# Gathered rows' buffers placed under the node stage, and relu of every second node tile on ScalarE, in a graph-network layer

## The chip, the cores and the metric

One core of one Trainium2 chip. The metric is the device time of one execution in microseconds; the kernel before took 4068.4 us, the median of three runs (4061.18 to 4073.2). The core's engines appear under the profile's names: PE (TensorE, matmuls; PEld its weight loads), DVE (VectorE), ACT (ScalarE), POOL (GpSimd) and SP (SyncE, which here only issues DMAs). A "q" behind a name (ACTq, SPq) is that engine's instruction queue, where DMA issues stand.

## The reference, cut to what matters

A message-passing layer over N = 12,500 nodes with 160 features (64 scalars and 32 vectors of 3) and E = 400,000 edges sorted by target.

```python
h = jnp.maximum(_layernorm(x, axis=-1), 0.0)
...
x0 = node_input[:, :MUL0]
x1 = node_input[:, MUL0:].reshape(n, MUL1, 3)
s0 = x0 @ W_sc0 * a * inv0
y0 = x0 @ W_l1_0 * a * inv0
y1 = jnp.einsum('nuc,uv->nvc', x1, W_l1_1) * a[:, :, None] * inv1
h = jax.nn.silu(edge_length_embedded @ fc_W1 * (1.0 / math.sqrt(FC_IN)))
w = h @ fc_W2 * (1.0 / math.sqrt(FC_H))
ys0 = y0[edge_src]
ys1 = y1[edge_src]
...
z0 = jnp.zeros((n, MID), mid0.dtype).at[edge_dst].add(mid0) * inv_nb
z1 = jnp.zeros((n, MID, 3), mid1.dtype).at[edge_dst].add(mid1) * inv_nb
...
return x + concat(C_S * s + C_X * (z @ W_l2) * a)
```

(The last line is shortened.) Each node's features are normalized and clipped at zero, then mapped by two weight matrices: s stays with the node, y is what neighbours read. Each edge gathers the y row of its source node, multiplies it by weights from a small network over the edge's attributes, and the products are summed at the target node. The division by the standard deviation is applied after the maps, as a factor on each row, so what has to be formed ahead of the maps is relu(x - mean) alone.

## The kernel before, in words

**Node stage (lines 267 to 410).** The 98 node tiles of 128 rows are worked in groups of 8 (GN), a group in steps of 2 tiles (HN). After them come 40 more tiles (RT), whose rows are not read in order but gathered from x into `xr` by the edges' source indices: they are the rows that 10 of the later edge blocks will need, mapped here a second time. They are called the reuse groups below. A step goes through seven stages, each some iterations behind the first: `center` (DVE: bn_stats, bn_aggr, then h = max(x - mean, 0), for either tile of the step; at the end of a group ACT takes the square root `ra` of the variances), `turn_rows` (PE transposes h), `out_of_psum` (ACT copies hT), `map_rows` (PE, two matmuls per tile), `leave` (ACT writes ys = po x ra; at the end of a group ACT issues the store of y to DRAM, `y_d` for the node groups and `yr_d` for the reuse groups), `scales` (DVE turns ra into its reciprocal times the node's attribute) and `add_s` (DVE adds s onto acc, L384, for the node groups). In one iteration q the stages are issued in the order scales(q-1), leave(q-4), out_of_psum(q-2), turn_rows(q-1), map_rows(q-3), center(q), add_s(q-5), and PE, ACT and DVE keep that order (`manual_schedule`). POOL and SP are ordered by the framework. On POOL lie the 80 gathers of `xr` and `ar` and the all-reduce L136 that finds the first target node of every window of edges.

**relate (lines 138 to 181).** DVE work of some 24 us on the edges' targets, after the last step. Its largest tile is `over`.

**Edge stage (lines 436 to 654).** 3125 edge tiles of 128 edges, in 782 blocks of 4. For a block b: `load(b)` gathers 4 x 128 rows of y_d into a buffer of the pool `yg` (POOL, one indirect DMA per tile, L474); every twelfth block from 12 to 120 is instead one plain load from yr_d, issued by SP (L471). `load` also issues, on SP, the edge attributes `xe` (L465), for every eighth block. `weigh` makes the edge weights (PE, then ACT scales them, L421), `select` and `products` (DVE, L427 to L434) multiply them with the gathered rows, `sums` (PE) adds up by target. A buffer of yg is free again when the products of its block have read it (L432 is the last to do so). Ten loads are issued ahead of the loop (AHEAD), then load(b + 10) in iteration b, and the pool has 12 buffers.

**Memory.** Pools are laid one upon the other in the order in which they are opened, and what a closed pool leaves is used again; whoever first writes to such memory waits for the last use of what lay there. Above the constants (from byte 114,912 of a partition on) lie, one after the other in time: idx, then the node stage's pools (xr at 138,528 to 164,128, the two ys buffers at 164,928 to 185,408), then relate's (over at 148,000 to 160,544, above idx), then the edge stage's (selp, prod, xe at 151,776 to 155,872, raw to 158,944, ev to 162,784, and yg at 162,784 to 193,504, 12 buffers of 2,560 bytes, then hid and post).

Of the kernel before, what the change touches and what calls it, by code (L numbers as in the profile page):

```python
# [10 lines left out]
F32 = mybir.dt.float32  # L11
I32 = mybir.dt.int32
AF = mybir.ActivationFunctionType
ALU = mybir.AluOpType
# [4 lines left out]
P = 128  # L19
# [26 lines left out]
def kernel(  # L46
# [19 lines left out]
    nc = tc.nc  # L66
# [51 lines left out]
    tile_i = const.tile([P, NG], I32, name="tile_i")  # L118
    far_i = const.tile([1, 1], I32, name="far_i")
    full = T // WT  # L120
    before = ctx.enter_context(ExitStack())
    ip = before.enter_context(tc.tile_pool(name="idx", bufs=1))
    dst_i = ip.tile([P, TP], I32, name="dst_i")
# [143 lines left out]
    with (  # L267
# [43 lines left out]
        def rows_of(g, n):  # L311
            return acc[:, g:g + n, :] if g < NT else xr[:, g - NT:g - NT + n, :]

        def center(q):

            g, n, j, m = steps[q]
            xt = rows_of(g, n)
            if j == 0:
                mvs[g] = ns.tile([P, GN, 2], F32, name="mv")
            mv = mvs[g]  # L320
            h = nd.tile([P, HN, D], F32, name="h")
            for k in range(m):
                st = ns.tile([P, 6], F32, name="st")
                nc.vector.bn_stats(st, xt[:, j + k, :])
                nc.vector.bn_aggr(mv[:, j + k, :], st)
                nc.vector.tensor_scalar(h[:, k, :], xt[:, j + k, :], mv[:, j + k, 0:1], 0.0, ALU.subtract, ALU.max)
            hs[q] = h
            if j + m == n:
                ra = ns.tile([P, GN], F32, name="ra")
                nc.scalar.activation(ra[:, :n], mv[:, :n, 1], AF.Sqrt, bias=eps)  # L330
                ras[g] = ra
# [55 lines left out]
        with tc.manual_schedule(engines=engines):  # L387
            load_x(0, HN)
            nc.sync.dma_start(a_sb, attr)
            node_weights()  # L390
            load_x(HN, min(GN, NT) - HN) if NT > HN else None
            nc.sync.dma_start(src_sb, src)
            for k, (g, n) in enumerate(groups[1:]):
                load_x(g, n)
                if k == 4:
                    nc.sync.dma_start(dst_i, dst)
            if len(groups) <= 5:
                nc.sync.dma_start(dst_i, dst)
            edge_weight_loads()
            last = len(steps) - 1  # L400
            mid = len(steps) - -(-RT // HN)
            for q in range(len(steps) + 5):
                if q == min(4, last) and RT:
                    gather_x()
                if q == min(16, mid):
                    first_nodes()
                for stage, lag in ((scales, 1), (leave, 4), (out_of_psum, 2), (turn_rows, 1), (map_rows, 3), (center, 0),
                                   (add_s, 5)):
                    if 0 <= q - lag <= last:
                        stage(q - lag)  # L410
# [25 lines left out]
    with (  # L436
# [1 line left out]
        tc.tile_pool(name="prod", bufs=3) as prod,  # L438
        tc.tile_pool(name="ld", bufs=2) as ld,
        tc.tile_pool(name="ev", bufs=2) as evp,  # L440
        tc.tile_pool(name="yg", bufs=12) as ygp,
        tc.tile_pool(name="hid", bufs=4) as hid,
        tc.tile_pool(name="post", bufs=2) as post,
        tc.tile_pool(name="p_w", bufs=2, space=PSUM) as p_w,
# [171 lines left out]
        with order:  # L616
# [10 lines left out]
            for b in range(NB):  # L627
                g, k = divmod(b, K)
# [30 lines left out]
    with (  # L659
# [11 lines left out]
        with tc.For_i(0, n, 1) as _:  # L671
            with tc.For_i(0, ZR, P) as r:
                nc.sync.dma_start(z_d[ds(r, P), :], zero)
            with tc.For_i(0, TP // GT, 1) as g:
# [15 lines left out]
                yg = fp.tile([P, GT, D], F32, name="f_yg")  # L690
# [102 lines left out]
```

## Time and profile before

| | |
|---|---|
| three runs | 4061.18, 4068.4, 4073.2 us |
| the profiled execution | 4061.72 us, of it span 4059.8 us |
| busy: PE, DVE, ACT, POOL | 3235.3, 2922.8, 2692.2, 3018.0 us (80, 72, 66, 74% of the span) |
| mean granted TensorE clock | 0.933 |
| node stage, first to last `center` | 11.9 to 166.3 us |
| relate on DVE | 166.8 to 190.8 us |
| first products on DVE | 208.0 us |
| gathers on POOL, first and last start | 175.2 and 4039.1 us |

How to read it: a group row gives the line, engine and operation, names (out<-in) and a count, then the busy time and the mean duration in ns, then the idle time of the engine just ahead of those instructions and what ended most of it. A row of the timeline gives the start, the busy time, engine, line and operation; in brackets stands the engine's idle time ahead of it and whom the profile names as the releaser. "issue" is time in which the engine waited for nothing that the profile shows. The releaser is inferred, and a wait for several things is put down to the one that came last. Rows of stretches of time give begin and end, the length, then the busy time of PE, PEld, DVE, ACT and POOL (with counts), the granted clock, the DMA engines' mean busy share, and GB/s.

### The profile page before, as it was taken

The numbers are of one execution on the slowest core, as the hardware profiler recorded it, in microseconds if no ns is written. First come the engines' busy times: TensorE is split into PE (matmuls) and PEld (weight loads), VectorE is DVE, ScalarE is ACT, GpSimd is POOL, SyncE is SP. The second block draws the span as 40 slices with busy tenths as digits, with TensorE's granted clock in tenths as the row PEclk, the third lists the DMA queues.
The fourth block names the chain that finished last, engine by engine and source line by source line (L and its number), as shares of the span: only waits on it lengthen the run. The fifth ranks groups of instructions, "written<-read, shape, count | busy, mean of one in ns | idle before, by whom it ended". The sixth has DMA issues, their size and how long they took to land.

```text
span 4059.8 us, 62554 instructions
## 1 busy us (share of the span) xinstructions
PE 3235.3 (80%) x17505; PEld 2347.5 (58%) x17505; DVE 2922.8 (72%) x7558; ACT 2692.2 (66%) x9543; POOL 3018.0 (74%) x3177
## 2 busy tenths in 40 slices
PE   6588888878787787887877887878777788778777
PEld 5466666555555555555555555555555555555555
DVE  7787777776777777777777777767777777777776
ACT  5477777766666666666666666666666666666665
POOL 7477777777777777777777777777777777777776
PEclk9899999999989989999999999999999989999998
DMA  6333333332322233323233332323232323243233
GB/s 192 88 84 83 80 83 80 76 76 74 77 74 74 74 76 74 77 74 76 72 76 75 75 76 74 74 74 77 74 76 74 76 72 76 75 124 75 72 81 78
DMA packets 244949, 326.49 MB, mean 80 GB/s; under 512 B 67290, under 2 KB 194342, under 8 KB 244342
## 3 DMA queue, kind: packets, MB, share of 16 engines
q0 software_dynamic: 151280, 256.22, 25.7%
q1 hardware_dynamic: 74322, 54.52, 4.7%
q10 hardware_dynamic: 18996, 11.72, 0.9%
q8 instruction: 141, 2.31, 0.2%
q14 instruction: 210, 1.72, 0.1%
HBM read 302.92 MB, written 19.28 MB: 79 GB/s over the span
## 4 chain that ended last, share of the span: by engine, by line
DVE 25%; POOL 23%; DMA 21%; issue 21%; PE 5%; ACT 1%; DVEq 1%; ACTq 0%; POOLq 0%
POOL yg L474 23%; DMA yg<-y_d,src_sb 21%; DVE tmp L429 5%; DVE tmp L427 5%; DVE pr L432 3%; DVE pr L431 2%; DVE acc L603 2%; DVE pr L434 2%; DVE sel L538 2%; PE pz L556 2%; DVE pr L430 2%; DVE sel L536 1%; PE pw L505 1%; PE px L483 1%; DVE place L586 1%
## 5 line engine op out<-in xcount | busy, mean ns | idle before, releaser
L474 POOL DMA_INDIRECT yg<-y_d,src_sb x3085 | 2925.3, 948 | 982.5 <-issue 745.8
L556 PE MATMUL pz<-pr,sel 128*128 128x256 f32 x6250 | 1623.9, 407 | 0.3 <-DVE pr L434 0.3
L421 ACT ACTIVATE pw<-pw,ev 128x96 f32<-128x96 f32 x3125 | 985.3, 315 | 858.3 <-PE pw L505 769.6
L556 PEld LDWEIGHTS pz<-pr,sel 128*128 128x128 f32 x6250 | 1237.4, 208 | 157.6 <-issue 0.9
L505 PE MATMUL pw<-w,hT 64*128 64x192 f32 x6250 | 758.5, 363 | 667.1 <-DVE pr L434 657.5
L427 DVE TENSOR_TENSOR tmp<-yg,pw 128x384 f32<-128x384 f32 x782 | 432.8, 553 | 972.3 <-DMA yg<-y_d,src_sb 970.8
L505 PEld LDWEIGHTS pw<-w,hT 64*128 64x128 f32 x6250 | 514.6, 194 | 1060.9 <-DVE pr L434 893.9
L563 ACT ACTIVATE zs<-pz 32x64 f32<-32x64 f32 x3126 | 669.9, 214 | 41.8
L429 DVE TENSOR_REDUCE tmp<-tmp 128x128 f32<-128x384 f32 x782 | 463.7, 593 | 27.0
L538 DVE TENSOR_TENSOR sel<-sel,pw 128x384 f32<-128x384 f32 x782 | 432.7, 553 | 27.0
L561 ACT ACTIVATE zs<-pz 32x192 f32<-32x192 f32 x1042 | 337.8, 324 | 148.3 <-PE pz L556 125.7
L432 DVE TENSOR_TENSOR pr<-pw,yg 128x384 f32<-128x384 f32 x782 | 428.8, 548 | 0.0
L483 PE MATMUL px<-xe,w 32*128 32x512 f32 x782 | 301.0, 656 | 81.8 <-issue 72.7
L488 ACT ACTIVATE hT<-px 128x512 f32<-128x512 f32 x391 | 218.5, 595 | 179.8 <-PE px L483 172.9
L431 DVE TENSOR_TENSOR pr<-pw,yg 128x256 f32<-128x256 f32 x782 | 324.1, 414 | 0.0
L430 DVE TENSOR_TENSOR pr<-pw,yg 128x256 f32<-128x256 f32 x782 | 323.8, 414 | 0.0
L536 DVE TENSOR_TENSOR sel<-iota,pw 128x128 f32<-128x128 f32 x782 | 218.8, 280 | 58.0 <-ACT pw L422 57.6
L580 PE MATMUL px<-wc,za 128*128 128x96 f32 (+1 forms) x1566 | 257.3, 305 | 0.4 <-ACT za L573 0.4
L580 PEld LDWEIGHTS px<-wc,za 128*128 128x128 f32 x1566 | 211.6, 205 | 62.2 <-issue 45.2
L434 DVE TENSOR_TENSOR pr<-pw,tmp 128x128 f32<-128x128 f32 x782 | 220.4, 282 | 0.0
L594 PE MATMUL px<-os,place 128*128 128x160 f32 x1044 | 219.0, 334 | 0.5 <-ACT os L583 0.5
L603 DVE SCALAR_TENSOR_TENSOR acc<-px,a_sb,acc 128x160 f32 x522 | 198.5, 380 | 12.2 <-PE px L594 2.7
(97 smaller groups left out, 1742.0 us busy)
## 6 DMA issues: line engine op xcount, KB each, us to landing
yg<-y_d,src_sb POOLq DMA_INDIRECT x3085
xe<-in_e SPq DMA_DIRECT2D x784, 32.0 KB
y_d<-ys ACTq DMA_DIRECT2D x12, 640.0 KB
acc<-in_x SPq DMA_DIRECT2D x11, 640.0 KB
out<-acc SPq DMA_DIRECT2D x11, 640.0 KB
raw<-in_e SPq DMA_DIRECT2D x32, 192.0 KB
yr_d<-ys ACTq DMA_DIRECT2D x5, 640.0 KB
yg<-yr_d SPq DMA_DIRECT2D x10, 320.0 KB
```

The costliest lines, as they stand in the source:

```text
L421: nc.scalar.activation(pw[:, k, 0:96], pw[:, k, 0:96], AF.Copy, scale=ev[:, k, 0:1])
L427: nc.vector.tensor_tensor(tmp[:, :n, 0:3, :], y1, wt[:, :n, NW:NW + 3].unsqueeze(3).to_broadcast([P, n, 3, M1]), ALU.mult)
L429: nc.vector.tensor_reduce(tmp[:, :n, 3, :], tmp[:, :n, 0:3, :].rearrange("p t c u -> p t u c"), AX.X, ALU.add)
L430: nc.vector.tensor_mul(pr[:, :n, 192:PC], wt[:, :n, 96:160], yg[:, :n, 0:M0])
L431: nc.vector.tensor_mul(pr[:, :n, 0:M0], wt[:, :n, 0:M0], yg[:, :n, 0:M0])
L432: nc.vector.tensor_mul(pr[:, :n, 96:192].rearrange("p t (c u) -> p t c u", c=3), wt[:, :n, M0:96].unsqueeze(2).to_broadcast([P, n, 3, M1]) ...
L474: nc.gpsimd.indirect_dma_start(out=yg[:, k, :], out_offset=None, in_=y_d, in_offset=bass.IndirectOffsetOnAxis(ap=src_sb[:, t:t + 1], axis=0))
L505: nc.tensor.matmul(pw[:, k, 0:NW], hT[r, o:o + P], w2[r, :], start=True, stop=True)
L538: nc.vector.tensor_tensor(sel[:, :, 0:3, :], sel[:, :, 3:4, :].to_broadcast([P, n, 3, WN]), wt[:, :n, NW:NW + 3].unsqueeze(3).to_broadcast ...
L556: nc.tensor.matmul(pz[:, 0:PC], sels[g][:, t % TG, :, :], pr[:, k, :], start=t % WT == 0, stop=last)
L563: nc.scalar.activation(zs[:, 192 + M0 * c:192 + M0 * (c + 1)], pz[WN * c:WN * (c + 1), 192:PC], AF.Copy)
L580: nc.tensor.matmul(po[:m, lo:hi], za[:, k, :m], wc[:, k, lo:hi], start=k == 0, stop=k == 1)
```

## The change

The pool `yg` is opened ahead of `idx` and so lies right above the constants for the whole program, under the memory of idx, the node stage and relate, which all move up by its 30,720 bytes. It no longer shares memory with any of them. In the edge stage selp, prod, ld and ev move up by the same 30,720 bytes; hid and post stay where they were. Nothing else of the gathers is touched.

In `center`, h of the first tile of a step stays on DVE. For the second tile DVE now writes `less`, the negated mean (128x1), and ACT computes relu(x + less). In the order of ACT it stands where `center` stands: behind leave(q-4) and out_of_psum(q-2), and ahead of the square root `ra`.

```diff
+    ygp = ctx.enter_context(tc.tile_pool(name="yg", bufs=12))
     before = ctx.enter_context(ExitStack())
     ip = before.enter_context(tc.tile_pool(name="idx", bufs=1))
...
                 nc.vector.bn_aggr(mv[:, j + k, :], st)
-                nc.vector.tensor_scalar(h[:, k, :], xt[:, j + k, :], mv[:, j + k, 0:1], 0.0, ALU.subtract, ALU.max)
+                if k % 2 == 0:
+                    nc.vector.tensor_scalar(h[:, k, :], xt[:, j + k, :], mv[:, j + k, 0:1], 0.0, ALU.subtract, ALU.max)
+                else:
+                    less = ns.tile([P, 1], F32, name="less")
+                    nc.vector.tensor_scalar(less, mv[:, j + k, 0:1], -1.0, None, ALU.mult)
+                    nc.scalar.activation(h[:, k, :], xt[:, j + k, :], AF.Relu, bias=less)
             hs[q] = h
...
         tc.tile_pool(name="ev", bufs=2) as evp,
-        tc.tile_pool(name="yg", bufs=12) as ygp,
         tc.tile_pool(name="hid", bufs=4) as hid,
```

## The prediction

> **What bounds the kernel now.** I read the chain of waits first, then the group of the gathers, then GpSimd's own timeline.
>
> ```profile
> DVE 25%; POOL 23%; DMA 21%; issue 21%; PE 5%; ACT 1%; DVEq 1%; ACTq 0%; POOLq 0%
> ...
> L474 POOL DMA_INDIRECT yg<-y_d,src_sb x3085 | 2925.3, 948 | 982.5 <-issue 745.8
> ...
> 175.21 1.47 POOL L474 DMA_INDIRECT yg<-y_d,src_sb  x1 [43.03 <-DVE lim L164]
> 176.99 4.06 POOL L474 DMA_INDIRECT yg<-y_d,src_sb  x1 [0.30 <-issue]
> ...
> 243.15 0.94 POOL L474 DMA_INDIRECT yg<-y_d,src_sb  x1 [0.30 <-DVE pr L432]
> ```
>
> No engine leads the chain, but the group row does: 3085 gathers of 0.948 us, each behind 0.30 us of issue, 1.25 us apart. 3085 x 1.25 is 3857 us; 175.2 + 3857 + 7.9 (the four slow ones at the start, 1.47, 4.06, 3.14 and 3.01 us instead of 0.95) is 4040, and the last gather starts at 4039.1. So GpSimd never rests from the first gather to the last; some 21 us of tail follow. The time is the start of the gathers, plus any stop among them, plus constants. Faster work elsewhere counts only if it moves one of these.
>
> The first gather came after 43 us of rest. The row names DVE's L164, a bystander by code: the gather reads y_d and src_sb and writes a yg buffer. Buffer 0 lies (162,784 to 165,344 in the layout) over the end of xr and the start of a ys buffer, and the last yr_d store reads that ys. The store and the DMA traffic by microseconds agree:
>
> ```profile
> 170.65 0.36 ACTq L378 DMA_DIRECT2D yr_d<-ys  x1
> ...
> 172.00:173.00 1.00, 0.00 (x0) 0.00 (x0) 0.92 (x4) 0.00 (x0) 0.00 (x0) 1.00 1.13 363
> 173.00:174.00 1.00, 0.00 (x0) 0.00 (x0) 0.97 (x3) 0.00 (x0) 0.00 (x0) 0.94 0.47 148
> 174.00:175.00 1.00, 0.00 (x0) 0.00 (x0) 0.95 (x3) 0.00 (x0) 0.00 (x0) 0.50 0.00 0
> ```
>
> The last two columns are DMA share and GB/s: the store drains in 173 to 174, the gather goes at 175.2.
>
> **Part 1, the buffers.** With yg under the node stage, the first gather needs only y_d. Its last store was issued at 134.47, and DMA traffic is nil from 138 on. So gathers could start near 138, 37 us sooner. Not all of it can be kept. There are 12 buffers: blocks 0 to 11 are 48 gathers, block 12 comes by SP, and gather 49 (block 13) needs the buffer of block 1, which products(1) must have read. That work doesn't move with the buffers:
>
> ```profile
> 190.81 7.33 SPq L465 DMA_DIRECT2D xe<-in_e  x16
> ...
> 212.92 0.55 DVE L432 TENSOR_TENSOR pr<-pw,yg 128x384 f32<-128x384 f32 x1
> ```
>
> xe (at 151,776) lies over the tile over (148,000 to 160,544), which relate reads until 190.7. yg was opened after xe, so both shift by the same 30,720 bytes and still overlap: SP still waits for relate. Products(1) still ends its reading at 213.5, and gather 49 starts at 213.8 with its 0.3 of issue. Before, gather 49 is the one at 243.15 (48 gathers start ahead of it). **Gain: 243.15 - 213.8 = 29.4 us.** The rest of the 37 becomes a new stop, on DVE's products.
>
> Are the 48 done by then? 138 + 48 x 1.25 + 7.9, and up to 3 more beside L152 and L166, which now also run beside gathers: 209. That leaves 4 us. The gathers also move past other work: DVE's h costs 0.30 alone and 0.39 to 0.40 now and then where the xr gathers run beside it (100 to 122 us), so the reuse steps may lose 0.1 in some of 20 steps, 1 us at most, left out of the sum; the loads of xr and ar (done by 122.8) and L136 (done by 132.2) stay ahead of them on GpSimd's queue. Do the consumers keep the lead? From 213.9 to 258.4 DVE starts 12 blocks, 3.7 us each; GpSimd needs 5.0 for a block (4.6 on average while every twelfth comes by SP). So they drain the backlog, and GpSimd stays the bound. If that cover went (PE's granted clock is 0.93 to 0.97 in this stretch, PE 88% busy from 243 to 420), a block would have to cost over 4.6 us before any is lost. The tail is unchanged.
>
> **Part 2, the relu.** It lies ahead of products(1): whatever the node stage gains or loses moves gather 49 one for one. Of 138 tiles 69 are odd. On DVE, h starts 0.22 us ahead of the next instruction; less replaces it. No row has it, so bounds: 0.13 (L181, 1x1) to 0.20 (L208); I take 0.165 between starts, nearest the 128x1 row of spare (0.15 busy). Saving 0.055, at most 3.8 us in all 69.
>
> ScalarE gains a relu of 128x160 from SBUF. Nearest is L373 in its 128x160 form: two in 0.68, the next instruction 0.57 after the first, so 0.29 between starts and 0.39 for one. Far bound: hT of 128x512, 0.48 between starts. The Trainium skill speaks against this part: ScalarE: Activation LUTs, Rules for kernel authors, wants relu on VectorE. Its formula for a pointer bias gives an estimate of 413 ns, 320 between starts: 0.03 more per relu than my row, some 1.4 us over all the groups.
>
> 0.29 would vanish if ScalarE had room. Does it, where a group of 8 tiles ends?
>
> ```profile
> 103.67 1.08 ACT L373 ACTIVATE ys<-po,ra 128x320 f32<-128x320 f32 x2 [1.50 <-PE po L362]
> 104.78 0.37 ACTq L376 DMA_DIRECT2D y_d<-ys  x1
> 105.19 0.60 ACT L352 ACTIVATE hT<-pt 128x512 f32<-128x512 f32 x1 [0.44 <-ACT ys L373]
> 105.68 0.29 ACT L330 ACTIVATE ra<-mv,eps 128x8 f32<-128x8 f32 x1
> ...
> 106.01 0.20 DVE L338 RECIPROCAL ra<-ra 128x8 f32<-128x8 f32 x1
> ```
>
> ScalarE works without a gap into ra, and DVE's reciprocal starts 0.04 after it. The slack there is zero; the 1.50 of rest lies earlier, waiting for PE, which waits for h. Now ScalarE can't run ahead of DVE, since it stands at relu until less comes, with ys, hT and the store's issue queued behind; PE's transposes of the odd tile wait for relu in turn, with the matmuls of an earlier step, which ys needs, behind them. I replay one group from the reciprocal at 106.01 (next one at 114.65), with measured spacings: L384 now ends early, the third step starts at 110.95 and less of the second step is out at 110.93. ScalarE: relu 110.98, ys 111.27, hT 112.10, relu 112.59, ys 112.88 (112.31 before), the store's issue 113.98, hT 114.39, relu 114.88, ra 115.17, done 115.47; reciprocal 115.50. **0.85 us lost in each group**. In the reuse groups (no L384, ys of 0.57 to 0.84, period 7.05) the same replay ends 0.65 to 0.83 late: 0.75.
>
> Sum: 10 full groups x 0.85 = 8.5; the first, the one that hides it behind first_nodes (44 to 50 us) and the two-tile one, 1.0 together; 5 reuse groups x 0.75 = 3.75: **13.3 us later**. Lower bound -3.8 (everything hidden, DVE's saving kept). Upper: relu at 0.48, three of them on a group's chain, +0.57 each group: 14.2 + 1.5 + 6.6 = 22. I take 13.3, by the nearer row. The y_d stores come 9.5 later too, so the 48 end by 219, against 227 for gather 49: still covered.
>
> **Total**: 29.4 - 13.3 = 16.1 us less. The profiled execution took 4061.7 (span 4059.8 and 1.9 around it): 4045.6. The three runs' median is 6.7 above it; the mean of the four is 4066.1. I forecast from that mean: **4050 us**.
>
> **Rivals.**
> A. *The relu is free.* For: ScalarE is busy 33 of the 50 us from 100 to 150. Against: no slack ahead of ra. 29.4 + 0 to 3.8: 4033 to 4037.
> B. *The lockstep eats more*, as PE also stands longer (transposes wait for two engines). For: relu now lies in the loop DVE, ScalarE, PE, ScalarE. At 18 to 25 us lost: 4055 to 4062, no change.
> C. *The start doesn't move*, the slower side: the first gather waits for something of relate after all, as its row says, and the relu's loss remains. For: the name L164. Against: the store's landing. 4066.1 + 13.3 = 4079. Gather 49 comes 68 us after the first (243.15 - 175.2), so the start decides from 159 on (227 - 68), and past 175.2 the kernel is slower. Of the same sign: L136's all-reduce put behind the gathers on GpSimd's queue, whose order isn't written by hand. It takes 9.4 (6.1 of rest and 3.3), each gather ahead of it 1.25, and products(1) end 47 us after relate begins (166.8 to 213.8): with over 31 ahead relate begins past 196 and the kernel is slower, with 48 by 30 us or more. Now it stands ahead of them, its input ready at 50.3.
> D. *Relu reloads the function table.* Two loads of 1.28 at each of 17 group ends: +44, so 4094. Against: Copy and Sqrt alternate from 18 to 171 us without a load. The skill (same page, Table sets) has relu in every set; no run here shows it yet.
>
> **Numbers.** Forecast 0.58, A 0.14, B 0.14, C 0.10 with its sister, D 0.04. Range 4034 to 4076: from A to most of C; the forecast's own range is 4043 to 4057. A measurement of this kernel tells 0.3%, 12.2 us, from no change. Faster: A and most of the forecast, 0.62. Same: the rest of it and B, 0.24. Slower: C and D, 0.14.
>
> **What would show it.** First L474 near 147, no longer 175. A rest of 5 to 10 us on GpSimd ahead of gather 49, at about 227, ended by DVE's L432; none after. Reciprocals of ra 9.5 us apart instead of 8.64, behind ra, behind relu. L141 near 180 instead of 166.8. Two table loads before 190. Gathers still 0.946. I am wrong if the first gather stays behind L164's time, if the reciprocals keep 8.6, or if GpSimd rests again after 300 us.

## The result, and the profile after

The changed kernel took 4048.41 us, the median of five runs (4046.89 to 4050.24), against 4068.4 before (five runs, 4061.18 to 4073.2). The ratio is 0.9952, with a 95% interval of 0.9937 to 0.9966: 19.5 us less, 14 to 26 by the interval. The forecast was 4050.

The profiled execution took 4048.41 us, of it span 4046.6. First the page's chain by engine and the group of the gathers (L480 now, L474 before):

```profile
DVE 23%; POOL 22%; DMA 21%; issue 20%; PE 6%; ACT 1%; DVEq 1%; ACTq 0%; POOLq 0%
...
L480 POOL DMA_INDIRECT yg<-y_d,src_sb x3085 | 2929.8, 950 | 968.5 <-issue 751.7
```

Little shows here: the chain's shares are within two points of those of before, and the gathers' idle time fell by 14 us net. What moved is seen on GpSimd's timeline, at the first gather, the 48th and the 49th (start, busy time, instruction, and in brackets the rest ahead of it):

```profile
145.25 1.19 POOL L480 DMA_INDIRECT yg<-y_d,src_sb  x1 [16.59 <-DMA y_d<-ys]
...
211.22 0.95 POOL L480 DMA_INDIRECT yg<-y_d,src_sb  x1 [0.30 <-issue]
224.26 0.94 POOL L480 DMA_INDIRECT yg<-y_d,src_sb  x1 [12.09 <-DVE pr L441]
```

The gathers start 30 us sooner, and what they wait for is now named as it is: the landing of the last y_d store. Then 48 of them run without a rest, and GpSimd stands for 12.1 us until DVE's products have freed a buffer. Gather 49 starts at 224.26 instead of 243.15: 18.9 us sooner. There is no rest after it. SP's loads of xe, which the first products need, and the last instruction that reads the buffer of block 1 (L471 and L439 in this kernel, L465 and L432 before):

```profile
201.48 7.33 SPq L471 DMA_DIRECT2D xe<-in_e  x16
...
223.44 0.55 DVE L439 TENSOR_TENSOR pr<-pw,yg 128x384 f32<-128x384 f32 x1
```

It ends at 223.99, and gather 49 starts 0.27 us later.

On ScalarE and DVE, the end of a group of 8 node tiles, timelines of the changed kernel (L333 is relu, L332 is less, L337 is ra, L345 the reciprocal):

```profile
98.97 0.43 ACT L333 ACTIVATE h<-acc,less 128x160 f32<-128x160 f32 x1 [1.17 <-DVE less L332]
99.31 0.93 ACT L380 ACTIVATE ys<-po,ra 128x320 f32<-128x320 f32 x2
100.13 0.59 ACT L359 ACTIVATE hT<-pt 128x512 f32<-128x512 f32 x1
100.61 0.43 ACT L333 ACTIVATE h<-acc,less 128x160 f32<-128x160 f32 x1
100.93 0.95 ACT L380 ACTIVATE ys<-po,ra 128x320 f32<-128x320 f32 x2
101.90 0.37 ACTq L383 DMA_DIRECT2D y_d<-ys  x1
102.32 0.60 ACT L359 ACTIVATE hT<-pt 128x512 f32<-128x512 f32 x1 [0.44 <-ACT ys L380]
102.81 0.42 ACT L333 ACTIVATE h<-acc,less 128x160 f32<-128x160 f32 x1
103.13 0.29 ACT L337 ACTIVATE ra<-mv,eps 128x8 f32<-128x8 f32 x1
...
101.81 0.15 DVE L332 TENSOR_SCALAR less<-mv 128x1 f32<-128x1 f32 x1
103.45 0.20 DVE L345 RECIPROCAL ra<-ra 128x8 f32<-128x8 f32 x1 [1.48 <-ACT ra L337]
```

ScalarE stands 1.17 us for less, and from there to ra it has no gap but that of the store's issue. DVE starts its last less at 101.81 (0.15 us) and then waits 1.48 us for ra. Reciprocals come 9.33 us apart, where they came 8.64 apart. Over the node stage DVE now waits 22.6 us for ra, where it waited 0.8.

### The profile page after: what moved, and what is told of

It is laid out like the page before. It is cut to its first block, busy times and chain, and to the rows that moved or that the text cites. A ratio compares the mean times of both kernels' runs of the same rounds, so it can differ in the third digit from the quotient of the medians.

```text
span 4046.6 us, 62656 instructions
## 1 busy us (share of the span) xinstructions
PE 3230.1 (80%) x17505; PEld 2346.9 (58%) x17505; DVE 2905.8 (72%) x7558; ACT 2709.6 (67%) x9612; POOL 3018.0 (75%) x3177
## 4 chain that ended last, share of the span: by engine, by line
DVE 23%; POOL 22%; DMA 21%; issue 20%; PE 6%; ACT 1%; DVEq 1%; ACTq 0%; POOLq 0%
POOL yg L480 22%; DMA yg<-y_d,src_sb 21%; DVE tmp L436 5%; DVE tmp L434 4%; DVE pr L439 3%; PE pz L562 3%; DVE pr L438 2%; DVE acc L609 2%; DVE sel L544 2%; DVE pr L441 2%; PE pw L511 1%; DVE pr L437 1%; DVE sel L542 1%; PE px L489 1%; ACT pw L428 1%
## 5 line engine op out<-in xcount | busy, mean ns | idle before, releaser
L480 POOL DMA_INDIRECT yg<-y_d,src_sb x3085 | 2929.8, 950 | 968.5 <-issue 751.7
L439 DVE TENSOR_TENSOR pr<-pw,yg 128x384 f32<-128x384 f32 x782 | 427.1, 546 | 0.0
L489 PE MATMUL px<-xe,w 32*128 32x512 f32 x782 | 292.8, 654 | 71.5 <-issue 61.4
```

The lines of the kernel that those rows point to most:

```text
L439: nc.vector.tensor_mul(pr[:, :n, 96:192].rearrange("p t (c u) -> p t c u", c=3), wt[:, :n, M0:96].unsqueeze(2).to_broadcast([P, n, 3, M1]) ...
L480: nc.gpsimd.indirect_dma_start(out=yg[:, k, :], out_offset=None, in_=y_d, in_offset=bass.IndirectOffsetOnAxis(ap=src_sb[:, t:t + 1], axis=0))
```

## The experiments

Each group of kernels ran on one chip, with the kernel before beside them; ratios are against the kernel before on that chip. Line numbers shift from kernel to kernel: the gather is L474 before and L475 to L487 below.

**yg_only: the buffers alone.**

```diff
+    ygp = ctx.enter_context(tc.tile_pool(name="yg", bufs=12))
...
-        tc.tile_pool(name="yg", bufs=12) as ygp,
```

> Only the pool yg is moved; relu of both tiles stays on VectorE. My theory: the node stage and relate stay as before (reciprocals of ra 8.64 us apart, relate from 166.8 to 190.8), the first gather starts near 138 (when the last y_d store has landed), gather 49 at 213.8 after a rest of GpSimd of some 5 us, ended by the products of block 1: 29.4 us less than before, ratio 0.9928, some 9 to 10 us less than both changes together. Rival 1 (the relu costs nothing and the start alone gave the 19 to 20 us): same time as both together, ratio 0.9952. Rival 2 (the first gather waits for something else of the node stage): first gather at 145 or later.

Ratio 0.9931 (0.9918 to 0.9945): 28 us of 4066.6. GpSimd's timeline of this kernel:

```profile
138.74 1.19 POOL L475 DMA_INDIRECT yg<-y_d,src_sb  x1 [5.74 <-DMA y_d<-ys]
...
205.57 0.95 POOL L475 DMA_INDIRECT yg<-y_d,src_sb  x1 [0.30 <-issue]
214.86 0.94 POOL L475 DMA_INDIRECT yg<-y_d,src_sb  x1 [8.35 <-DVE pr L436]
```

First gather 138.7 (138 expected), gather 49 at 214.9 (213.8), reciprocals 8.63 apart. Both rivals fell: the move alone is worth 28 us, not 19, and the gathers wait for y_d, not for relate. The 1.1 us over my figure come from relate, which starts 1.0 later than in the profile of before (167.84 against 166.80; xe is issued at 192.00 instead of 190.81). Reuse groups take 7.15 to 7.19 beside the gathers instead of 7.06, which is some 0.3 of it. What makes the rest isn't shown; before_again, below, shows a shift of that size without any change.

**relu_only: the relu alone**, with yg where it lay.

```diff
-                nc.vector.tensor_scalar(h[:, k, :], xt[:, j + k, :], mv[:, j + k, 0:1], 0.0, ALU.subtract, ALU.max)
+                if k % 2 == 0:
...
+                    nc.scalar.activation(h[:, k, :], xt[:, j + k, :], AF.Relu, bias=less)
```

> Only the relu of the second tile of a step is moved to ScalarE; yg lies where it lay before. My theory: reciprocals 9.33 us apart instead of 8.64, the last yr_d store and with it the first gather 10.5 us later (near 186), no stop at gather 49, everything after 10.5 us later: ratio 1.0026. Rival 1 (relu is free): ratio 1.000. Rival 2 (VectorE's saving of 0.15 us in each odd tile shows once the gathers don't run beside the node stage): below 1.000.

Ratio 1.0022 (1.0013 to 1.0031): 9 us slower. Its first gather, and two reciprocals:

```profile
185.65 1.48 POOL L479 DMA_INDIRECT yg<-y_d,src_sb  x1 [57.30 <-DVE lim L164]
...
103.18 0.20 DVE L343 RECIPROCAL ra<-ra 128x8 f32<-128x8 f32 x1 [1.47 <-ACT ra L335]
112.51 0.20 DVE L343 RECIPROCAL ra<-ra 128x8 f32<-128x8 f32 x1 [1.48 <-ACT ra L335]
```

The first gather is 10.4 us later (185.65 against 175.21), the groups 9.33 apart. The row names L164 again, though here L164 lies 10 us later too. It is a bystander: in yg_only the gathers run ahead of relate and so need nothing that it makes, and in the trace of before GpSimd's wait for the last yr_d store ended at 174.12, as that store's semaphore was full (174.06), while L164 ran to 174.89. The same wait ended at 184.56 here, 1.1 us ahead of the gather, as before. At gather 49 the two parts add up: 28.3 sooner (214.86 against 243.15) and 10.4 later make 17.9, where both together gave 18.9.

**before_again: the kernel before, profiled once more**, for a question that the result raised. Gather 49 came 18.9 us sooner, but the profiled spans differ by 13.2: the gathers from the 49th on took 1.2522 us each instead of 1.2503.

> The kernel before, unchanged, for a second profile of it. Gathers 49 to 3085 took 3796.0 us in its profile and 3801.7 us in the profile of the changed kernel, 1.2503 and 1.2522 us each, which ate 5.7 us of the 18.9 by which gather 49 came sooner. Theory: the pace differs from one execution to the next, whatever the kernel; here it may be anywhere from 1.250 to 1.253. Rival: the new addresses of yg slow the gathers; then the pace here is 1.2503 again, and that of yg_only 1.2522.

Its pace is 1.2516 (gather 49 at 245.29, the last at 4045.17, 3036 steps) and its time 4067.7. With yg moved, yg_only had 1.2515; relu_only, with the old place of yg, 1.2503. Four more kernels with yg moved, further below, had 1.2500 to 1.2503. So the pace goes with the execution and not with the place of the buffers; the rival fell.

This second profile also shows how far the start of relate moves by itself (166.80 in the first profile):

```profile
168.90 1.24 DVE L141 TENSOR_REDUCE first<-negb 128x261 f32<-128x1044 f32 x1
```

Its first gather starts at 177.31 instead of 175.21, and gather 49 at 245.29 instead of 243.15. So differences of 2 us at gather 49 between two profiles can't by themselves be put down to an edit.

**both_later, both_ra_first, both_13, yg_order, on another chip.** Four kernels, each with one thing altered. both_later makes relu a stage of its own, one step later:

```diff
-                for stage, lag in ((scales, 1), (leave, 4), (out_of_psum, 2), (turn_rows, 1), (map_rows, 3), (center, 0),
-                                   (add_s, 5)):
+                for stage, lag in ((scales, 1), (leave, 5), (out_of_psum, 3), (relu, 1), (turn_rows, 2), (map_rows, 4),
+                                   (center, 0), (add_s, 6)):
```

> Both changes, but relu is a stage of its own one step behind center, ahead of which ScalarE has less already in hand; the transposes, copies, maps, stores and sums follow one step later. The same instructions in number and size on every engine, only the order differs. My theory (the loss came from ScalarE standing in order at relu until less comes, and ra behind it): VectorE doesn't wait for ra any more and keeps its 0.15 us in each odd tile, reciprocals 8.0 to 8.3 us apart, relate ends some 14 to 18 us sooner than with both changes as they were (201.3), gather 49 at 206 to 211 instead of 224.3, ratio 0.990 to 0.992. Rival (ScalarE simply has too much work with relu in it): reciprocals stay near 9.3, ratio 0.995.

both_ra_first issues the last relu of a group behind ra:

```diff
             if j + m == n:
                 ra = ns.tile([P, GN], F32, name="ra")
                 nc.scalar.activation(ra[:, :n], mv[:, :n, 1], AF.Sqrt, bias=eps)
                 ras[g] = ra
+            if m > 1:
+                nc.scalar.activation(h[:, 1, :], xt[:, j + 1, :], AF.Relu, bias=less)
```

> Both changes, and in the last step of a group the square root ra stands ahead of relu in ScalarE's order. My theory: of the 0.69 us that a group lost, the 0.32 of the last relu go, since the reciprocal starts after ra: reciprocals 9.0 apart instead of 9.33, gather 49 some 5 us sooner, near 219, ratio 0.994. Rival (the loss is all in the wait for less in mid-group): 9.33 stays, ratio 0.9952. Rival (ra is all of it): 8.6, ratio 0.992.

both_13 has `bufs=13` for yg.

> Both changes, and 13 buffers of yg instead of 12. My theory (the stop ahead of gather 49 is the wait for a free buffer): block 13 now takes the buffer of block 0, which is free 3.2 us sooner than that of block 1, so gather 49 starts at 221.1 instead of 224.3 and the whole is 3.2 us shorter, ratio 0.9944 against 0.9952, at the edge of what can be told by time; the profile decides. Rival (the stop is something else, as the gathers' index or the DMA queue): gather 49 stays at 224.

yg_order leaves relu on DVE and opens the edge stage's pools in another order:

```diff
+        tc.tile_pool(name="post", bufs=2) as post,
         tc.tile_pool(name="ld", bufs=2) as ld,
         tc.tile_pool(name="ev", bufs=2) as evp,
         tc.tile_pool(name="hid", bufs=4) as hid,
-        tc.tile_pool(name="post", bufs=2) as post,
```

> yg moved, relu left on VectorE, and in the edge stage the pool post opened ahead of ld, ev and hid, so that xe, raw, ev and the hidden tiles no longer lie over the tile over of relate, but over xr and ys, which are free some 15 us sooner. My theory (the rest ahead of gather 49 comes from xe, which waits for over): SP issues xe near 176 to 178 instead of 192, products of block 0 start near 198 instead of 209, GpSimd has no rest at gather 49, which starts at 207 instead of 214.9: 8 us less than with yg alone, ratio 0.991. Rival (xe waits for relate's result and not for memory): xe at 192 as before, ratio 0.993.

On this chip the kernel before took 5912 us as well (35 runs, 5884.9 to 5948.3), at a mean granted clock of 0.77. Ratios: both_later 1.0034 (1.0012 to 1.0056), both_ra_first 1.0035 (1.0007 to 1.0064), both_13 1.0017 (0.9997 to 1.0037), yg_order 1.0001 (0.998 to 1.0021). As times they decide nothing on the theories. The longest waits of yg_order there (us in total, times, longest):

```profile
POOL yg L475 <- DVE pr L436: 1796.4, 282, 61.6
DVE acc L604 <- remote: 1379.6, 164, 10.5
ACT pw L423 <- remote: 1011.9, 154, 11.1
```

At the two lines shown engines stood again and again, for up to 11 us, for something that the profile can't name ("remote"), and GpSimd stood 282 times for a free buffer. The gathers themselves had their usual median step of 1.25 us. Where the gathers wait for their consumers all along, as here, a sooner start was worth nothing. Why this chip did so stays open.

In its quiet stretches the node stage still answers one question. Reciprocals of both_ra_first:

```profile
177.81 0.20 DVE L346 RECIPROCAL ra<-ra 128x8 f32<-128x8 f32 x1 [1.13 <-ACT ra L336]
186.82 0.20 DVE L346 RECIPROCAL ra<-ra 128x8 f32<-128x8 f32 x1 [1.14 <-ACT ra L336]
```

9.01 apart, as expected, where both_13, with relu ahead of ra, has 9.33 on this chip too: 0.32 of the 0.69 us that a group lost is the relu ahead of ra. Its effect on the whole wasn't measured on an undisturbed chip. The other three were run again, on a chip where the kernel before took 4061.6 us.

**both_later_b.**

> The kernel of both_later once more, since the time of that run (5912 us for the kernel before as well) says nothing on this. As there: reciprocals 8.0 to 8.3 apart (8.05 in that run), xe issued near 184 instead of 201.5, gather 49 at 206 to 211 after a rest of some 5 us, ratio 0.990 to 0.992. Rival (too much work for ScalarE): 9.3 and 0.995.

Ratio 0.9910 (0.9897 to 0.9924). ScalarE and DVE at the end of a group, and gather 49:

```profile
88.06 0.66 ACT L366 ACTIVATE hT<-pt 128x512 f32<-128x512 f32 x1
88.53 0.50 ACT L345 ACTIVATE h<-acc,less 128x160 f32<-128x160 f32 x1
89.78 0.30 ACT L338 ACTIVATE ra<-mv,eps 128x8 f32<-128x8 f32 x1 [0.75 <-DVE mv L328]
...
90.11 0.20 DVE L352 RECIPROCAL ra<-ra 128x8 f32<-128x8 f32 x1 [0.18 <-ACT ra L338]
...
205.53 0.95 POOL L487 DMA_INDIRECT yg<-y_d,src_sb  x1 [8.22 <-DVE pr L448]
```

The same instructions, and now ScalarE waits for DVE ahead of ra, not DVE for ScalarE. Groups are 8.05 to 8.2 apart, faster than with relu on DVE (8.64), and xe goes out at 182.89. Gather 49 starts 18.7 us sooner than in the changed kernel, even before the 206 to 211 that I expected. The rival fell: ScalarE has room for the relu; what cost was its place in the order.

**yg_order_b.**

> The kernel of yg_order once more, for the same reason. My theory (the rest ahead of gather 49 comes from xe, which waits for over): xe near 176 to 178 instead of 192, no rest of GpSimd at gather 49, which starts at 207 instead of 214.9, ratio 0.991. Rival (xe waits for relate's result): xe at 192, ratio 0.993.

Ratio 0.9908 (0.9893 to 0.9923). SP's xe and gather 49:

```profile
176.68 3.60 SPq L466 DMA_DIRECT2D xe<-in_e  x8
...
207.99 0.94 POOL L475 DMA_INDIRECT yg<-y_d,src_sb  x1 [0.30 <-issue]
```

xe goes 15 us sooner and the rest ahead of gather 49 is gone: in yg_only it came from xe lying over `over`, as the forecast had it.

**both_13_b.**

> The kernel of both_13 once more, for the same reason. My theory (the stop is the wait for a free buffer): gather 49 at 221.1 instead of 224.3. Rival: 224.3 stays.

Ratio 0.9947 (0.9932 to 0.9962), not to be told from 0.9952 by time. Gather 49, and L439 of blocks 0 and 1, the last to read their buffers:

```profile
222.69 0.94 POOL L480 DMA_INDIRECT yg<-y_d,src_sb  x1 [11.24 <-DVE pr L441]
...
221.87 0.55 DVE L439 TENSOR_TENSOR pr<-pw,yg 128x384 f32<-128x384 f32 x1
225.07 0.55 DVE L439 TENSOR_TENSOR pr<-pw,yg 128x384 f32<-128x384 f32 x1
```

Gather 49 follows block 0 now, and not block 1, which is read until 225.6. It is only 1.6 us sooner than in the changed kernel because SP took 8.44 us for the xe issues here and 7.33 there, and started them 0.5 later. The stop is the wait for a free buffer.

**later_order: the best of these**, yg moved, relu a step later, and the pools in the new order.

> All three together: yg moved, relu of the second tile on ScalarE as a stage of its own one step behind center, and post opened ahead of ld, ev and hid. My theory, from reciprocals 8.05 us apart where relu is a step later: y_d is complete near 133, the first gather starts at 134, relate ends near 184, products of block 1 near 196, GpSimd finds the buffer of block 1 free and has no rest at gather 49, which starts near 203 instead of 243.15 or 224.3: ratio 0.990. Rival (what the node stage wins is lost in a new rest ahead of gather 49 or later): no better than yg alone, 0.993.

4015.65 us against 4061.63, ratio 0.9886 (0.9871 to 0.9901): 46 us less, ahead of both kernels. GpSimd around the first gather, and gather 49:

```profile
125.64 3.33 POOL L138 PARTITION_ALL_REDUCE negb<-neg  x1 [6.13 <-DVE ra L352]
129.20 1.57 POOL L487 DMA_INDIRECT yg<-y_d,src_sb  x1 [0.23 <-issue]
...
196.64 0.94 POOL L487 DMA_INDIRECT yg<-y_d,src_sb  x1 [0.30 <-DVE sel L551]
```

It beat my figures (203, ratio 0.990), mostly since the first gather comes at 129 and not 134. GpSimd has no rest from there to its last gather. What is late next stands in the same lines: the first gather follows the all-reduce at once (the last y_d store was issued at 125.66), so y_d no longer sets the start, but GpSimd's own queue does.

## Why the prediction was right

- **The bound.** GpSimd paced by 1.25 us from the first gather on, and only start and stops count: held. In the changed kernel one stop, none after it.
- **The start.** Near 138 with the node stage unslowed: 138.74 in yg_only, released by the y_d store. The mechanism held; that the figure is so near is in part luck. The store was issued at 136.32 there, 1.9 us later than in the first profile of before, and the gather followed 2.4 us later, where 3.5 had been allowed. With both changes the first gather came at 145.25 (147 forecast).
- **The new stop.** Gather 49 on the products of block 1, which wait for xe, which lies over `over`: held in each link. yg_order_b took xe out and the rest went; both_13_b moved the wait from block 1 to block 0. The gain of this part was put at 29.4 and is 28.3 against the first profile of before, 30.4 against the second. The rest itself was 12.1 us and not the 5 to 10 of the forecast (8.35 in yg_only, not 5): the first 48 gathers took 66.9 us, where 71 had been put, as the slow ones among them cost about 7 us and not 7.9 and 3 more. This changed nothing for the time, since the products set gather 49.
- **The relu.** ScalarE standing in order, ra behind relu, and VectorE waiting for it: held (relu_only, both_later_b, both_ra_first). The size was off. The term was 13.3 us and measured 8.3 to 10.4 at gather 49: 10.4 and 8.3 for relu_only against the two profiles of before, 9.4 for the changed kernel against yg_only. A full group lost 0.69 instead of 0.85, a reuse group 0.51 instead of 0.75 (7.57 in relu_only, 7.06 before). Laid beside the replay, the group of the changed kernel that is shown above (reciprocal at 94.12, the next at 103.45) has three prices that were wrong.
  - less holds DVE for 0.07 us, not the 0.165 that was taken from the busy times of small instructions. Its own busy time is 0.15 us, so a busy time doesn't say when the next may start. So the relu of the second step starts 4.86 us behind the reciprocal instead of 4.97, 0.11 sooner. The rest of what DVE saved (0.15 us in each odd tile, 10.3 in all 69, instead of 3.8) didn't shorten the group: it went into the wait for ra.
  - The relu took 0.43 us and 0.32 to 0.34 between starts, not 0.39 and 0.29; the estimate from the Trainium skill (ScalarE: Activation LUTs, What ACT_TABLE_LOAD costs), 413 and 320 ns, was the nearer one here. Three of them on the chain make 0.10 more.
  - From the last pair of ys to the store's issue the replay took 1.10 from the profile of before, where the second ys starts 0.55 behind the first. In the changed kernel it starts 0.41 behind it, and the issue follows at 0.98: 0.13 less.

  The first two nearly cancel, which is luck; the third is most of the 0.15 by which the group came out shorter than in the replay.
- **The rule against it.** Rules for kernel authors, on the same page of the skill, want relu on VectorE. As the change placed it the rule was right, by 8 to 10 us. Placed a step later the relu on ScalarE was the better one: gather 49 at 205.5 in both_later_b and 214.9 in yg_only, with relu on VectorE. The engine's price per element didn't decide this, the order did.
- **The sum.** 16.1 us expected, 18.9 by gather 49, 20.0 by the medians, 13.2 from profile to profile. The last is short by the 5.7 us of pace: the profiled execution of before was a fast one. That 4050 came so near 4048.4 is in part luck: the gain was put 3 to 4 us too low, and the mean of the four executions, from which the forecast was made, lay 2.3 below the median of five.
- **The rivals.** A fell (the relu costs 8 to 10), B fell short (it would have needed 18), C fell with yg_only, its sister too: the all-reduce still stands ahead of the gathers (125.33 and 145.25 in the changed kernel). D fell: two table loads of 1.28 us before 200 us, as before; relu needed none of its own beside Sqrt and Copy, which agrees with the Trainium skill (ScalarE: Activation LUTs, Table sets), where relu is in every set.

## What to carry to other kernels

Where one queue is busy from its first instruction to its last, the time is its start plus its stops: give its buffers memory of their own, and then look at once for what empties the first of them, since a sooner start only turns into a wait there. When work is handed to an engine that runs in a written order, put it where its input is already there; the same instructions cost 9 us in one place and saved 9 in another (gather 49 at 224.26 and at 205.53, against 214.86 with relu on VectorE). And such a gain holds only while that queue is the bound: where its consumers stood still for other reasons, it was worth nothing.

## What was not expected of the hardware

The gathers' pace differs from one execution to another by nearly as much as the relu cost here: 1.2500 to 1.2522 us in the nine profiles on the other chips (1.2503, 1.2516 for the kernel before), over 3036 gathers a difference of 6.7 us, with a median step of 1.25 us in all of them. What makes it is open. And one chip took at least 45% longer for every kernel of which there is a time on another, with unnamed waits of up to 11 us at two lines of DVE and ScalarE; that too is open.
